# The first scan's causal convolution on TensorE instead of VectorE, an operand's product moved to GpSimd, and an earlier tail for the scan's last chunk

## Chip, cores and metric

The kernel runs on one core of one Trainium2 chip. The time is the device time of one execution in microseconds, as the median of several runs.

## What is computed

The input x is 32 sequences of 256 tokens of 256 features, all float32. A conditioning block with a recurrent scan is applied first; then two layers of windowed attention and a gated feed-forward follow, and x is added at the end. The change touches only the conditioning block, which per sequence is:

```python
xr, gate = jnp.split(x @ W_in.T, 2, axis=-1)          # 512 channels each
xr = xr + t_emb[:, None, :]
xc = causal_depthwise_conv(xr, W_conv, taps=4) + b_conv
xc = silu(xc)
xn = layernorm(xc) * ln_g + ln_b
Bm, Cm, dt = jnp.split(xn @ W_xproj.T, 3, axis=-1)     # 16 states each
dt = jnp.tanh(dt @ W_dt.T + b_dt) * 0.01
Ad = 1.0 + dt * (-jnp.tanh(A_log))
Bd = Bm * jnp.minimum(norm(xn), 1.0)
def step(h, inputs):                                   # 256 steps, one after the other
    ad, bd, xt, ct = inputs
    h = jnp.clip(h * ad[:, :, None] + bd[:, :, None] * xt[:, None, :], -10.0, 10.0)
    return h, jnp.einsum('bd,bdh->bh', ct, h)
y = ys.transpose(1, 0, 2) + D * xn
return y * silu(gate) @ W_out.T
```

## The kernel before, in words

**Groups and the mix.** The sequences are worked on in four groups of eight (`GB = 8`). The scan of group 0 runs first, with no attention beside it; the code calls this `alone`. After it, the attention and feed-forward of group g run beside the scan of group g+1, and the last group's attention runs with no scan beside it.

**Slots.** A group's scan is written as an agenda: `at(s, what, ...)` puts a piece of work into slot s, and slot t holds step t of the scan. Work for a chunk c of 32 tokens (`CH = 32`, so eight chunks) is placed relative to `s0 = 32 c`: its projection at s0-40 and on, `conv_in`, `conv_taps` and `conv_out` of its four channel blocks at s0-38 to s0-29, the layer norm around s0-24, the figures (decay, input and output factors) at s0-11 to s0-5, and the output of chunk c after its steps. The four channel blocks' convolutions of chunk c+1 therefore lie between six slots before the first step of chunk c and its step 3. The agenda gives the order in which instructions are recorded; a scheduler with a model of its own then orders each engine's queue, and each queue runs in order.

**One step.** For step t the row of xn is spread over 128 partitions (16 states x 8 sequences) into a tile `xrep` of two tokens. In the first scan two tokens of four are spread by TensorE (`bx`, L632) and two are read by a DMA (L624); in later groups all are read by DMA. ScalarE multiplies by `beta` (L643), VectorE makes the clipped sum into a new state tile `h` (L650, 512 elements wide), and TensorE sums the states for the output (`y`, L662, four steps at a time). The three `xrep` buffers (`xp`, `bufs=3`) tie a load to the step three tiles earlier.

**The convolution.** `conv_in` (L428) adds the condition to the projection in PSUM and writes `xr` (L437, VectorE); GpSimd makes tap 0 with the bias, `acc` (L443). `conv_taps` (L451) adds taps 1 to 3 by three VectorE operations in place (L454) and ScalarE takes the tanh (L459). `conv_out` writes `xc` (L464, VectorE). `figures` (L551) makes its matmul operand `rhs` on VectorE (L558), twice for each chunk.

**The output.** After the last step of a half chunk (`hb`), `gated` (L711) adds the skip, `out_turn` (L717) transposes on TensorE, `out_gate` (L731) multiplies by the gate, `project_y` (L740) makes eight products, `copy_y` (L751) and `put_y` (L760) store into DRAM scratch `ys`. Attention starts when `load_res` (L864) has read `ys` back.

**PSUM.** All matmul results come from one pool of eight banks (`ps_w`, tag `w`).

**The hand-over.** The last lines of `program` record the scan up to slot S + 17 (`DRAIN = 17`), then the eight `load_res`, then six projections of the first sequence with one more slot each; from there scan slots are dealt out over the attention's stages by a formula that starts from the slot reached (`s0`) and ends at slot 2S + 17.

Of the kernel before, what the change touches and what calls it, by code (L numbers as in the profile page):

```python
# [35 lines left out]
TAPS = 4  # L36
# [16 lines left out]
def bc(ap, axis, n):  # L53

    ap = ap.unsqueeze(axis)
    shape = list(ap.shape)
    shape[axis] = n
    return ap.broadcast_to(shape)
# [15 lines left out]
def kernel(  # L74
# [29 lines left out]
    nc = tc.nc  # L104
# [33 lines left out]
    wc_sb = loaded(w_conv, [P, NC_, TAPS], "wc_sb")  # L138
    bconv_sb = loaded(b_conv, [P, NC_], "bconv_sb")
# [5 lines left out]
    ident = const.tile([P, P], FP, tag="ident", name="ident")  # L145
# [10 lines left out]
    tok_step = sums("tok_step", CH, ident.rearrange("p (b t) -> p t b", b=BJ))  # L156
# [6 lines left out]
    for j in range(NJ):  # L163
# [18 lines left out]
        out=mask_t[:, 0:W], in_=mask_t[:, 0:W], compare_op=ALU.is_ge, fill=MASKED_LOW,  # L182
# [3 lines left out]
        out=mask_t[:, W : 2 * W], in_=mask_t[:, W : 2 * W], compare_op=ALU.is_ge,  # L186
# [29 lines left out]
    for i in range(2):  # L216
        t = const.tile([P, NI * (P + GB)], FP, tag=f"ly{i}", name=f"ly{i}")
# [3 lines left out]
    def program(ctx, exact):  # L221
        rpool = ctx.enter_context(tc.tile_pool(name="res", bufs=1, reuse_waits="tile"))
        wpool = ctx.enter_context(tc.tile_pool(name="weights", bufs=1, reuse_waits="tile"))
        sp = ctx.enter_context(tc.tile_pool(name="sp", bufs=1, reuse_waits="tile"))
# [8 lines left out]
        def bank(pool, tag, name):  # L233
            return pool.tile([P, DI], FP, tag=tag, name=name)
# [150 lines left out]
        def group_scan(g):  # L385
# [7 lines left out]
            b0 = g * GB  # L393
            alone = g == 0

            agendas = [{}]
            state = {"p": one}
            ck = [{} for _ in range(NCH)]

            def at(s, what, *args):  # L400
                agendas[-1].setdefault(s, []).append(partial(what, *args))
# [26 lines left out]
            def conv_in(c, ch):  # L428
                if ch == 0:
                    ck[c]["xc"] = sp.tile([P, NC_, GB * CH], FP, tag="xc", name="xc")  # L430
                ps = ck[c].pop(("ps", ch))
                xr = sp.tile([P, GB, TAPS - 1 + CH], FP, tag="xr", name="xr", bufs=2)
                if c == 0:
                    nc.gpsimd.memset(xr[:, :, 0 : TAPS - 1], 0.0)
                else:
                    nc.gpsimd.tensor_copy(xr[:, :, 0 : TAPS - 1], ck[c - 1]["carry"][:, ch])
                nc.vector.tensor_add(  # L437
                    xr[:, :, TAPS - 1 :],
                    ps.rearrange("p (b t) -> p b t", b=GB),
                    bc(cond_sb[:, ch, b0 : b0 + GB], 2, CH),  # L440
                )
                acc = sp.tile([P, GB, CH], FP, tag="acc", name="acc", bufs=2)
                nc.gpsimd.tensor_scalar(  # L443
                    acc, xr[:, :, 0:CH], wc_sb[:, ch, 0:1], bconv_sb[:, ch : ch + 1],
                    ALU.mult, ALU.add,
                )
                if c < NCH - 1:
                    nc.gpsimd.tensor_copy(ck[c]["carry"][:, ch], xr[:, :, CH:])
                ck[c]["xr", ch] = xr, acc

            def conv_taps(c, ch):  # L451
                xr, acc = ck[c]["xr", ch]
                for k in range(1, TAPS):
                    nc.vector.scalar_tensor_tensor(  # L454
                        acc, xr[:, :, k : k + CH], wc_sb[:, ch, k : k + 1], acc,
                        ALU.mult, ALU.add,
                    )
                th = sp.tile([P, GB * CH], FP, tag="th", name="th", bufs=2)
                nc.scalar.activation(th, acc.rearrange("p b t -> p (b t)"), AF.Tanh, scale=0.5)  # L459
                ck[c]["th", ch] = th  # L460

            def conv_out(c, ch):
                _, acc = ck[c].pop(("xr", ch))
                nc.vector.scalar_tensor_tensor(  # L464
                    ck[c]["xc"][:, ch], ck[c].pop(("th", ch)), 1.0,
                    acc.rearrange("p b t -> p (b t)"), ALU.add, ALU.mult,
                )


# [81 lines left out]
            def figures(c):  # L551
                stat = ck[c].pop("stat")
                pst = bank(ps_w, "w", "ps_st")[:, 0 : 3 * CH].rearrange(
                    "p (i t) -> p i t", i=3
                )
                for j in range(NJ):
                    rhs = sm.tile([P, 3, CH], FP, tag="rhs", name="rhs")
                    nc.vector.tensor_mul(rhs, bc(tok_step, 1, 3), bc(stat[:, j], 2, CH))  # L558
                    nc.tensor.matmul(
                        pst,  # L560
                        sel[:, j].rearrange("p n b -> p (n b)"),
                        rhs,
                        start=(j == 0),
                        stop=(j == NJ - 1),
                    )
                ck[c]["pst"] = pst
# [208 lines left out]
                )  # L775
                rep_w.append(t)

            rep_w = []
            at(-1, start)
            if alone:  # L780
                at(-30, spread_weights)
                constants(at)
            for c in range(NCH):
                for t in range(CH):
                    at(c * CH + t, step, c, t)
            for c in range(NCH):
                s0 = c * CH
                for hb in range(CH // TB):
                    s = s0 + hb * TB
                    for i in range(NI):  # L790
                        at(s + 4 * i + 5, read_out, c, hb, i)
                    at(s + 21, gated, c, hb)
                    at(s + 24, out_gate, c, hb)
                    at(s + 11, skip, c, hb)
                for ch in range(NC_):
                    at(s0 - 38 + 2 * ch, conv_in, c, ch)
                    at(s0 - 37 + 2 * ch, conv_taps, c, ch)
                    at(s0 - 35 + 2 * ch, conv_out, c, ch)
                for ch, s in enumerate((13, 16, 17, 18)):
                    at(s0 + s + 1, gate_th, c, ch)  # L800
                    at(s0 + s + 2, gate_out, c, ch)
                at(s0 - 24, raw_copy, c)
                at(s0 - 23, raw_turn, c)
                for j in range(NJ):
                    s = s0 - 24 + 4 * j
                    at(s + 2, norm_stats, c, j)
                    at(s + 4, norm_apply, c, j)
                    at(s + 5, norm_affine, c, j)
                    at(s + 8, norm_out, c, j)
                at(s0 - 11, length, c)  # L810
                at(s0 - 7, figures_in, c)
                at(s0 - 5, decays, c)
                at(s0 - 4, put_c, c, 0)
                at(s0 + 4, put_c, c, 1)
                for d in range(KM):
                    at(s0 + 44 + 2 * d, copy_y, c, d)
                    at(s0 + 45 + 2 * d, put_y, c, d)
            agendas.append({})
            for c in range(NCH):
                s0 = c * CH  # L820
                at(s0 - 43, load_x, c)
                for ch in range(NC_):
                    at(s0 - 40 + 2 * ch, project, c, ch)
                for ch, s in enumerate((13, 16, 17, 18)):
                    at(s0 + s, project, c, NC_ + ch)
                at(s0 - 26, raw_sums, c)
                for j in range(NJ):
                    at(s0 - 24 + 4 * j, norm_turn, c, j)
                at(s0 - 9, figures, c)
                for t in range(CH):  # L830
                    if t % XR == 0:
                        at(s0 + t - 5, load_rows, c, t)
                    if by_tensor(t) and t % XR == 0:
                        at(s0 + t - 4, spread_rows, c, t)
                    at(s0 + t - 2, scale_row, c, t)
                for hb in range(CH // TB):
                    s = s0 + hb * TB
                    at(s - 9 if alone else s + 7, load_skip, c, hb)
                    at(s + 22, out_turn, c)
                for d in range(KM):  # L840
                    at(s0 + 42 + 2 * d, project_y, c, d)

            return agendas

# [507 lines left out]
        def scan_to(s):  # L1352
            while done[0] is None or done[0] < s:
                done[0] = next(scan, 1 << 30)


        DRAIN = 17
        for i, (kind, k) in enumerate(WEIGHTS):
            scan_to(100 + 8 * i)
            load_weights(0, kind, k)  # L1360
        scan_to(S + DRAIN)
        for b in range(GB):
            load_res(0, b)
        for w in range(NW):
# [135 lines left out]
```

## Time and profile before

| what | value |
|---|---|
| median of 3 runs | 3995.38 us (3995.34, 3995.38, 4005.80) |
| the profiled execution | 4008.98 us |
| its span in the profile | 4007.1 us |
| TensorE busy over the span | 3794.7 us (95%) |
| VectorE busy | 2634.7 us (66%) |
| ScalarE busy | 2327.0 us (58%) |
| GpSimd busy | 1758.9 us (44%) |

The profile's rows name an engine (PE is TensorE, PEld its weight loads, DVE VectorE, ACT ScalarE, POOL GpSimd, SP the engine whose queue issues most DMAs), a source line, the operation, output tile <- input tiles, and a count. In a table of stages each pair `a (xn)` is busy microseconds and instructions of one engine; the last three columns are the clock granted to TensorE, the share of DMA time, and GB/s. A float32 matmul leaves two records, so a count of 8 is four matmuls; a transpose leaves one. A row of the timeline starts with its start and its length in microseconds, and merges equal instructions that follow each other, so its length can hold idle time.

### The profile page before, as it was taken

How to read it: one execution, taken by the hardware profiler on the slowest of the kernel's cores; microseconds unless marked ns; L12 is line 12 of the kernel's file. 1: busy time of each engine (PE TensorE's matmuls, PEld its weight loads, DVE VectorE, ACT ScalarE, POOL GpSimd, SP SyncE). 2: the span in 40 equal slices, each digit the busy share in tenths (PEclk: the TensorE clock that was granted, in tenths of full speed). 3: DMA queues.
4: the chain of work that ended last, by engine and by line, in shares of the span. 5: the costliest groups of instructions: out<-in, count | busy, mean ns of one | idle time of the engine just before them, and what ended most of it. 6: DMA issues, size and time to landing. Idle time of an engine off the chain costs nothing.

```text
span 4007.1 us, 57108 instructions
## 1 busy us (share of the span) xinstructions
PE 3794.7 (95%) x20540; PEld 2375.0 (59%) x20540; DVE 2634.7 (66%) x5241; ACT 2327.0 (58%) x3895; POOL 1758.9 (44%) x1784
## 2 busy tenths in 40 slices
PE   7888889999999899999999999999999999999999
PEld 3333345666666565666666666666666666666666
DVE  6888877777777666676676767666666544444443
ACT  3555546666666566666666666656666554455453
POOL 4443365444444444454444445444444444334341
PEclk8899989999999999999999999999999999999999
DMA  5444543333433435333343444333343111000000
GB/s 151 111 115 114 147 120 95 99 103 99 118 104 99 119 101 123 90 86 102 85 113 98 109 114 120 100 77 102 95 106 98 43 32 44 1 16 20 20 11 23
DMA packets 295896, 353.43 MB, mean 88 GB/s; under 512 B 166627, under 2 KB 213044, under 8 KB 295476
## 3 DMA queue, kind: packets, MB, share of 16 engines
q1 hardware_dynamic: 211154, 337.68, 31.9%
q10 hardware_dynamic: 84450, 12.01, 2.0%
q8 instruction: 165, 2.70, 0.3%
q14 instruction: 127, 1.04, 0.1%
HBM read 314.49 MB, written 33.55 MB: 87 GB/s over the span
## 4 chain that ended last, share of the span: by engine, by line
PE 55%; DVE 8%; POOL 7%; ACT 6%; DMA 5%; issue 3%; ACTq 0%; SPq 0%; POOLq 0%; DVEq 0%
PE ps_qkv L893 11%; PE pa L1224 9%; PE po_f L1247 8%; DMA xrep<-xnd 5%; PE ov L1137 4%; PE sc L1099 3%; PE ps_wo L943 3%; PE y L662 3%; DVE h L650 2%; PE ps_in L407 2%; PE rb L1152 2%; PE rs L1118 2%; POOL rn L925 2%; PE tr_qk L932 2%; PE ps_out L740 1%
## 5 line engine op out<-in xcount | busy, mean ns | idle before, releaser
L650 DVE CUSTOM_DVE_ANT_0 h<-h,xrep,lim 128x512 f32<-128x512 f32 x1024 | 926.3, 905 | 87.1 <-ACT xrep L643 31.8
L643 ACT ACTIVATE xrep<-xrep,beta 128x512 f32<-128x512 f32 x896 | 613.6, 718 | 546.0 <-DMA xrep<-xnd 455.9
L893 PE MATMUL ps_qkv<-qkv,res 128*128 128x512 f32 x1536 | 709.8, 598 | 1.7 <-DMA res<-ys 1.5
L1224 PE MATMUL pa<-hT,w 128*128 128x256 f32 (+1 forms) x3072 | 692.5, 387 | 2.3 <-ACT xn L527 1.7
L917 POOL TENSOR_TENSOR rot<-rot,swp 128x512 f32<-128x512 f32 x256 | 334.0, 1305 | 757.2 <-DVE swp L914 604.5
L1224 PEld LDWEIGHTS pa<-hT,w 128*128 128x128 f32 (+1 forms) x3072 | 498.2, 178 | 210.8 <-issue 68.4
L925 POOL TENSOR_TENSOR rn<-ss,neg_half 128x8 f32<-128x8 f32 x256 | 439.7, 1718 | 23.6 <-DVE ss L923 13.0
L893 PEld LDWEIGHTS ps_qkv<-qkv,res 128*128 128x128 f32 x1536 | 277.3, 190 | 273.6 <-issue 244.9
L1235 DVE SCALAR_TENSOR_TENSOR ag<-pa,b_sb,ag 128x256 f32<-128x256 f32 (+1 forms) x448 | 212.5, 475 | 298.1 <-ACT ag L1232 296.1
L662 PE MATMUL y<-h,ly 128*32 128x512 f32 x2048 | 367.3, 623 | 25.2 <-DVE h L650 23.1
L1247 PE MATMUL po_f<-ag,w 128*128 128x256 f32 (+1 forms) x1536 | 382.4, 390 | 2.0 <-DVE ve L1185 1.3
L1247 PEld LDWEIGHTS po_f<-ag,w 128*128 128x128 f32 (+1 forms) x1536 | 276.5, 189 | 112.2 <-issue 54.5
L926 POOL TENSOR_TENSOR rot<-rot,rn 128x512 f32<-128x512 f32 x256 | 291.4, 1138 | 19.7
L407 PE MATMUL ps_in<-xg,w_in_sb 128*128 128x256 f32 x1024 | 287.7, 409 | 11.1 <-DMA xg<-in_xT_dram 11.0
L1108 ACT ACTIVATE pT<-sc 128x512 f32<-128x512 f32 x384 | 208.3, 594 | 145.4 <-PE sc L1099 144.1
L407 PEld LDWEIGHTS ps_in<-xg,w_in_sb 128*128 128x128 f32 x1024 | 186.5, 196 | 161.9 <-issue 80.1
L909 DVE TENSOR_TENSOR rot<-ps_qkv,rc_sb 128x512 f32<-128x512 f32 x256 | 175.8, 687 | 152.7 <-ACT sq L906 152.5
L454 DVE SCALAR_TENSOR_TENSOR acc<-xr,wc_sb,acc 128x256 f32<-128x256 f32 x384 | 189.5, 495 | 101.4 <-POOL acc L443 99.9
L1108 ACT ACT_TABLE_LOAD x186 | 238.6, 1283 | 19.0 <-PE sc L1099 12.9
L1232 ACT ACT_TABLE_LOAD x187 | 239.9, 1283 | 6.4 <-issue 2.1
L943 PE MATMUL ps_wo<-oT,wo 128*128 128x256 f32 x1024 | 232.0, 380 | 0.0
L1099 PE MATMUL sc<-qT,kT 64*128 64x128 f32 (+1 forms) x2048 | 219.6, 343 | 0.0
(149 smaller groups left out, 5601.7 us busy)
## 6 DMA issues: line engine op xcount, KB each, us to landing
xrep<-xnd SPq DMA_DIRECT2D x448, 512.0 KB
xnd<-xn SPq DMA_DIRECT2D x64, 256.0 KB
qkv<-in_wqkv_dram SPq DMA_DIRECT2D x24, 512.0 KB
xd<-xnd SPq DMA_DIRECT2D x192, 64.0 KB
w<-in_w_dram SPq DMA_DIRECT2D x80, 128.0 KB
xg<-in_xT_dram SPq DMA_DIRECT2D x64, 128.0 KB
ys<-yo ACTq DMA_DIRECT2D x64, 128.0 KB
res<-ys SPq DMA_DIRECT2D x32, 256.0 KB
```

What stands on the lines that cost most here:

```text
L407: nc.tensor.matmul(ps, w_in_sb[:, k, ch * P : (ch + 1) * P], ck[c]["xg"][:, k], start=(k == 0), stop=(k == KM - 1),)
L643: nc.scalar.activation(bx, ck[c].pop(("bx", t), bx), AF.Copy, scale=ck[c]["beta"][:, t : t + 1])
L650: nc.vector._custom_dve(TENSOR_ADD_SAT, out=h_new, in0=state["h"], in1=bx, s0=ck[c]["lim"][:, 0, t : t + 1], s1=ck[c]["lim"][:, 1, t : t + 1],
L662: nc.tensor.matmul(ck[c]["y", hb][32 * q : 32 * q + 32, :], ly[hb % 2][:, 32 * t : 32 * t + 32], ck[c].pop(("h", hb * TB + t)), start=(i = ...
L893: nc.tensor.matmul(ps, res[b][:, k, t0 : t0 + W], wt["qkv", a][:, k], start=(k == 0), stop=(k == KM - 1),)
L917: nc.gpsimd.tensor_add(rot, rot, swp)
L925: nc.gpsimd.tensor_tensor(rn, ss, neg_half, ALU.pow)
L943: nc.tensor.matmul(po[:, d], wt["wo", 0][:, c, d * P : (d + 1) * P], oT[:, c, :], start=(c == 0), stop=(c == NC_ - 1),)
L1099: nc.tensor.matmul(banks[r][:, i, :], kT[rows, i0 + i, kw * W : (kw + 1) * W], qT[rows, i0 + i, kw * W :], start=False, stop=(i == n - 1),)
L1108: nc.scalar.activation(p, banks[r], AF.Exp)
L1224: nc.tensor.matmul(pg if x else pa, wt["w1", m][:, k, x], self.h[:, k], start=(k == 0), stop=(k == KM - 1),)
L1247: nc.tensor.matmul(self.po[:, d], wt["w2", 0][r0 : r0 + n, m, d * P : (d + 1) * P], self.ag[m][r0 : r0 + n], start=(m == 0), stop=(m == le ...
```

## The change

Four things are changed.

1. In the first scan only (`alone`), `conv_taps` becomes five accumulating matmuls into a PSUM bank: one of a row of biases with a row of ones, and one for each of four taps, whose weights are a 128 x 128 diagonal of that tap's 128 channel weights. The tanh and `conv_out` read the PSUM bank. GpSimd's tap 0 and VectorE's three taps are gone there; `acc` has no SBUF tile. The diagonals are built once, by two VectorE products of 1024 elements (`tap_weights`); the bias row is loaded by a DMA of 512 single elements on ScalarE's queue and the ones by a GpSimd memset (`tap_bias`). They live in the buffers of the three `qkv` weights.
2. In all groups, `rhs` is made by GpSimd.
3. For the last half of the last chunk of the first scan (`end`), `gated`, `out_turn`, `out_gate`, `project_y`, `copy_y` and `put_y` are placed 3 to 9 slots earlier, and the eight `load_res` are recorded after slot S + 7 instead of S + 17.
4. The weights are loaded in another order: `wo`, `w1`, `w2` recorded from slot 64 on, the three `qkv` at slot S - 30, because their buffers hold the diagonals until then.

```diff
+            def end(c, hb):
+                return alone and c == NCH - 1 and hb == CH // TB - 1
...
-                acc = sp.tile([P, GB, CH], FP, tag="acc", name="acc", bufs=2)
-                nc.gpsimd.tensor_scalar(
-                    acc, xr[:, :, 0:CH], wc_sb[:, ch, 0:1], bconv_sb[:, ch : ch + 1],
-                    ALU.mult, ALU.add,
-                )
+                if alone:
+                    acc = None
+                else:
...
             def conv_taps(c, ch):
-                xr, acc = ck[c]["xr", ch]
-                for k in range(1, TAPS):
-                    nc.vector.scalar_tensor_tensor(
-                        acc, xr[:, :, k : k + CH], wc_sb[:, ch, k : k + 1], acc,
-                        ALU.mult, ALU.add,
-                    )
+                xr, acc = ck[c].pop(("xr", ch))
+                if alone:
+                    acc = bank(ps_w, "w", "ps_conv")[:, 0 : GB * CH]
+                    nc.tensor.matmul(
+                        acc,
+                        tap_w[2][0:1, 0, ch * P : (ch + 1) * P],
+                        tap_w[2][0:1, 1, 0 : GB * CH], start=True, stop=False
+                    )
+                    for k in range(TAPS):
+                        nc.tensor.matmul(
+                            acc.rearrange("p (b t) -> p b t", b=GB),
+                            tap_w[ch // KM][:, ch % KM, k * P : (k + 1) * P],
+                            xr[:, :, k : k + CH],
+                            start=False,
+                            stop=(k == TAPS - 1),
+                        )
+                else:
...
-                    nc.vector.tensor_mul(rhs, bc(tok_step, 1, 3), bc(stat[:, j], 2, CH))
+                    nc.gpsimd.tensor_mul(rhs, bc(tok_step, 1, 3), bc(stat[:, j], 2, CH))
...
+            def tap_weights(i):
+                t = wpool.tile([P, KM, DI], FP, tag=f"qkv{i}", name="tap_w")
+                nc.vector.tensor_mul(
+                    t.rearrange("p c (k n) -> p c k n", k=TAPS),
+                    bc(bc(ident, 1, TAPS), 1, KM),
+                    bc(wc_sb[:, i * KM : (i + 1) * KM], 3, P),
+                )
+                tap_w.append(t)
+            def tap_bias():
+                t = wpool.tile([P, KM, DI], FP, tag="qkv2", name="tap_b")
+                nc.scalar.dma_start(
+                    out=t[0:1, 0].rearrange("p (c n) -> p c n", c=NC_),
+                    in_=b_conv.rearrange("p c -> c p").unsqueeze(0),
+                )
+                nc.gpsimd.memset(t[0:1, 1], 1.0)
+                tap_w.append(t)
...
+                for i in range(NC_ // KM):
+                    at(-41, tap_weights, i)
+                at(-41, tap_bias)
...
-                    at(s + 21, gated, c, hb)
-                    at(s + 24, out_gate, c, hb)
+                    at(s + (21, 18)[end(c, hb)], gated, c, hb)
+                    at(s + (24, 19)[end(c, hb)], out_gate, c, hb)
...
-                    at(s0 + 44 + 2 * d, copy_y, c, d)
-                    at(s0 + 45 + 2 * d, put_y, c, d)
+                    at(s0 + (44 + 2 * d, 37 + d)[end(c, 1)], copy_y, c, d)
+                    at(s0 + (45 + 2 * d, 37 + d)[end(c, 1)], put_y, c, d)
...
-                    at(s + 22, out_turn, c)
+                    at(s + (22, 18)[end(c, hb)], out_turn, c)
...
-                    at(s0 + 42 + 2 * d, project_y, c, d)
+                    at(s0 + (42 + 2 * d, 36)[end(c, 1)], project_y, c, d)
...
-        for i, (kind, k) in enumerate(WEIGHTS):
-            scan_to(100 + 8 * i)
+        for i, (kind, k) in enumerate(WEIGHTS[3:] + WEIGHTS[:3]):
+            scan_to(S - 30 if kind == "qkv" else S // 4 + 8 * i)
             load_weights(0, kind, k)
-        scan_to(S + DRAIN)
+        scan_to(S + 7)
```

More of the change, by code (lines that the diff above doesn't have):

```diff
@@ L441, in conv_in @@
                 )
-                acc = sp.tile([P, GB, CH], FP, tag="acc", name="acc", bufs=2)
-                nc.gpsimd.tensor_scalar(
-                    acc, xr[:, :, 0:CH], wc_sb[:, ch, 0:1], bconv_sb[:, ch : ch + 1],
-                    ALU.mult, ALU.add,
-                )
+                if alone:
+                    acc = None
+                else:
+                    acc = sp.tile([P, GB, CH], FP, tag="acc", name="acc", bufs=2)
+                    nc.gpsimd.tensor_scalar(
+                        acc, xr[:, :, 0:CH], wc_sb[:, ch, 0:1], bconv_sb[:, ch : ch + 1],
+                        ALU.mult, ALU.add,
+                    )
                 if c < NCH - 1:
@@ L451, in conv_taps @@
             def conv_taps(c, ch):
-                xr, acc = ck[c]["xr", ch]
-                for k in range(1, TAPS):
-                    nc.vector.scalar_tensor_tensor(
-                        acc, xr[:, :, k : k + CH], wc_sb[:, ch, k : k + 1], acc,
-                        ALU.mult, ALU.add,
-                    )
+                xr, acc = ck[c].pop(("xr", ch))
[5 more added lines that the diff above has]
+                        tap_w[2][0:1, 1, 0 : GB * CH], start=True, stop=False
+                    )
+                    for k in range(TAPS):
[7 more added lines that the diff above has]
+                else:
+                    for k in range(1, TAPS):
+                        nc.vector.scalar_tensor_tensor(
+                            acc, xr[:, :, k : k + CH], wc_sb[:, ch, k : k + 1], acc,
+                            ALU.mult, ALU.add,
+                        )
+                    acc = acc.rearrange("p b t -> p (b t)")
                 th = sp.tile([P, GB * CH], FP, tag="th", name="th", bufs=2)
-                nc.scalar.activation(th, acc.rearrange("p b t -> p (b t)"), AF.Tanh, scale=0.5)
-                ck[c]["th", ch] = th
+                nc.scalar.activation(th, acc, AF.Tanh, scale=0.5)
+                ck[c]["th", ch] = th, acc
             def conv_out(c, ch):
-                _, acc = ck[c].pop(("xr", ch))
+                th, acc = ck[c].pop(("th", ch))
                 nc.vector.scalar_tensor_tensor(
-                    ck[c]["xc"][:, ch], ck[c].pop(("th", ch)), 1.0,
-                    acc.rearrange("p b t -> p (b t)"), ALU.add, ALU.mult,
+                    ck[c]["xc"][:, ch], th, 1.0, acc, ALU.add, ALU.mult
                 )
@@ L776, in spread_weights @@
                 rep_w.append(t)
-            rep_w = []
+            def tap_weights(i):
[11 more added lines that the diff above has]
+                    in_=b_conv.rearrange("p c -> c p").unsqueeze(0),
+                )
+                nc.gpsimd.memset(t[0:1, 1], 1.0)
+                tap_w.append(t)
+            rep_w, tap_w = [], []
             at(-1, start)
```

## The prediction, as put on record

> **What bounds the kernel now.** I read the table of stages first, to see where the kernel has idle time (columns: span, busy time and count of PE, PEld, DVE, ACT, POOL; granted clock, DMA share, GB/s):
>
> ```profile
> 47.00:98.00 51.00, 46.90 (x153) 17.21 (x153) 44.70 (x89) 28.44 (x53) 23.83 (x30) 0.94 0.47 128
> 199.50:250.30 50.80, 45.09 (x172) 18.09 (x172) 43.23 (x81) 29.06 (x55) 21.68 (x33) 0.90 0.45 115
> 301.00:352.00 51.00, 45.67 (x172) 18.09 (x172) 43.98 (x81) 28.55 (x54) 19.93 (x25) 0.90 0.45 114
> 900.00:1300.00 400.00, 386.83 (x2208) 249.32 (x2207) 295.74 (x582) 256.11 (x433) 182.92 (x189) 1.00 0.41 105
> 3260.00:4007.00 747.00, 738.68 (x4224) 509.12 (x4222) 309.02 (x684) 362.05 (x567) 275.49 (x235) 1.00 0.07 19
> ```
>
> From about 600 us to the end TensorE is busy 97 to 99% of the time and bounds the kernel; nothing taken from VectorE is worth anything there. The first scan (53 to 460 us) is different. One of its chunks of 32 steps takes 50.8 us (189 steps in 300 us), and PE and DVE are both busy 85 to 90%. The chain that ended last shows nothing ahead of 640 us, so I look at the groups of instructions of 150 to 450 us, shapes kept apart:
>
> ```profile
> L650 DVE CUSTOM_DVE_ANT_0 h<-h,xrep,lim 128x512 f32<-128x512 f32 x189 | 162.2, 858 | 13.6 <-ACT xrep L643 6.7 <-PE ps_out L740 1.0
> L662 PE MATMUL y<-h,ly 128*32 128x512 f32 x378 | 101.5, 645 | 6.9 <-DVE h L650 5.9
> L454 DVE SCALAR_TENSOR_TENSOR acc<-xr,wc_sb,acc 128x256 f32<-128x256 f32 x70 | 34.1, 488 | 7.3 <-POOL acc L443 7.3
> L443 POOL TENSOR_SCALAR acc<-xr,wc_sb,bconv_sb 128x256 f32<-128x256 f32 x23 | 29.9, 1300 | 45.0 <-DVE xr L437 44.7
> L558 DVE TENSOR_TENSOR rhs<-tok_step,stat 128x96 f32<-128x96 f32 x11 | 8.8, 832 | 0.0
> L607 POOL TENSOR_TENSOR ly<-ct,st_seq 128x128 f32<-128x128 f32 x12 | 7.8, 651 | 6.2 <-PE y L662 5.7
> L643 ACT ACTIVATE xrep<-xrep,beta 128x512 f32<-128x512 f32 x94 | 63.9, 718 | 31.9 <-DMA xrep<-xnd 31.9
> ```
>
> PE's 90% is not work alone: `y` is busy for 101 us because it waits for the next `h` between its matmuls. The waits of 0 to 450 us (total, times, longest) have it, and two stretches of the timeline (start, length) show where:
>
> ```profile
> PEld y L662 <- DVE h L650: 56.1, 51, 2.5
> ```
>
> ```profile
> 213.61 4.34 PE L662 MATMUL y<-h,ly 128*32 128x512 f32 x8 [1.08 <-DVE h L650]
> ...
> 220.34 1.13 PE L632 MATMUL bx<-xq,rep_w 32*128 32x512 f32 x4
> 221.40 0.66 PE L503 MATMUL tp_x<-ident,xc 128*128 128x128 f32 x4
> 221.98 1.05 PE L662 MATMUL y<-h,ly 128*32 128x512 f32 x4
> 222.97 3.72 PE L740 MATMUL ps_out<-zT,w_out_sb 128*128 128x256 f32 x16
> 226.62 1.13 PE L632 MATMUL bx<-xq,rep_w 32*128 32x512 f32 x4
> ...
> 228.26 1.07 PE L662 MATMUL y<-h,ly 128*32 128x512 f32 x8
> 229.26 1.99 PE L407 MATMUL ps_in<-xg,w_in_sb 128*128 128x256 f32 x8
> ```
>
> Each row from 220.34 on starts where the one before ends: from 217.9 to 237.9 us, 20 us of each chunk, PE has no wait, and 14 steps pass at 1.34 us. In the other 30.8 us, where the convolutions lie, 18 steps take 1.71 us each, four `y` that need 1.07 us take 4.34 us, and PE waits for DVE. So the first scan has a PE-limited and a DVE-limited stretch, and the change moves work from DVE to PE in the second.
>
> [...] the eight `ps_out` matmuls of 256 columns take 3.65 us to the next start, 0.456 each[...]. [...] `rhs` has a median of 253 ns in the mixed part, but 832 ns on average here, where a GpSimd product of 1.26 us starts 0.06 us ahead of it.
>
> **The change, part by part.** The sum is made against the profiled execution's own 4008.98 us (span 4007.1 and 1.9 around it), which lies 13.6 us above the median of 3995.38; the difference is then taken from the median.
>
> *Taken from DVE, per chunk.* Twelve `acc` of 0.488 us: 5.86, less about 0.09 each that overlaps its neighbours: 4.8. Their wait for GpSimd's `acc`: 7.3 us in 5.9 chunks, 1.2. Two `rhs`: 1.48 us in the timeline, 1.4. Sum 7.4 us. GpSimd loses four `acc` (5.2 us) and gains two `rhs`. Their GpSimd time isn't in the trace: at least the 0.25 us that DVE needs, at most the 0.65 of the larger `ly` product; I take 0.5. GpSimd was busy 20 of 51 us and has room; the product now directly follows the GpSimd power that it needs, so no hand-over is added.
>
> *Put on PE, per chunk.* Four groups of five matmuls of 256 columns: 20 x 0.43 = 8.6 us. PE's own work per chunk, from start to start in the timeline: 16 `bx` in pairs of 1.06, 8 `y` groups of 0.99, 8 `ps_in` of 0.97, `ps_out` 3.65, `ps_raw` 1.87, transposes 2.4, `ps_st` 1.1: 33.2 us; 41.8 after. The 20 us stretch is PE-limited already and gets none of either. The other has 13.2 us of PE work before and 21.8 after; with a clock of 0.95, between the 0.90 of here and the 1.00 of the busy part, 23 us. DVE's need there falls from 30.8 to 23.4. The two are level, so waits between them now show. In the changed order on PE a channel's projection stands one or two groups ahead of its convolution, with DVE's `xr` between: up to one `h` (0.8) and `xr` (0.42) and hand-overs, less the bias matmul (0.43), about 0.8 us each, 3.2 per chunk (bounds 0 and 8.6: nothing, or every group in full). 23.4 + 3.2 = 26.6, and the chunk is 46.6: 4.2 us less, of at most 7.4. Queued behind a waiting convolution are `bx` and `y`; who waits for them is ScalarE's scaling, two slots later, then the step. The tanh and `xc` read PSUM instead of SBUF; I take no change. The group's bank comes from the eight in use; its own wait for a bank is within the 3.2.
>
> *How often.* Chunks 1 to 7 have their convolution beside steps: 7 x 4.2 = 29.4. Chunk 0's is in the start-up, and beside chunk 7 lies group 1's, which stays on DVE; there only `rhs` goes: 1.4.
>
> *Start-up.* Two DVE products of 1024 elements[...]. DVE has nothing to do from about 7 to 13.5 us, waiting for x: hidden[...]. The bias DMA is behind four others on ScalarE's queue, is issued near 9 us, and is needed at 13.9 us: hidden if it lands within 4 us. Chunk 0 itself trades 12 `acc` for 20 matmuls at a clock of 0.76: 8.6/0.76 = 11.3 us on PE against 14 us from the first `xr` to the last `xc` before, PE's other work coming on top: I take 2 us lost (from -2 to +6).
>
> *Weights.* The `qkv` loads (1.5 MB) were issued at 10 us and now stand in SP's queue among the `xrep` loads of the last chunks. An `xrep` load of 512 KB lands 4.7 to 5.2 us after issue. Behind three such loads one load may be late by up to 8 us; I take 2 us lost (0 to 8). `wo`, `w1`, `w2` still lead the queue.
>
> *Tail.* Before, the last `ys` store is issued at 483.6, the first `res` load at 487.6, the first `ps_qkv` at 491.2. The order on DVE has 278 steps ahead of the first attention product before, 270 after. Eight steps of 1.55 us come off: 12.4. They are done later, in the PE-bound part, at (33.2 - 8.5 for `bx`)/32 = 0.77 us of PE each: 6.2 back. Net 6.2 (0 to 12).
>
> *Mixed part.* `rhs` on GpSimd for 24 more chunks: DVE isn't the bound there, GpSimd is under half busy; taken as 0.
>
> Sum: 29.4 + 1.4 - 2 - 2 + 6.2 = 33 us. The profiled execution would be 3976, the median **3962 us**.
>
> **Rivals.** *DVE's relief passes in full* (no waits between the two): 7 x 7.4 + 1.4 - 4 + 6.2 = 55: 3940. [...] Against: 21.8 us of matmuls in a stretch of 23.4. *PE or the row loads take the place of DVE* (the clock stays at 0.90; or `xrep` lands later: issue, 5 us to land and 0.72 to scale must fit in five steps, 1.2 us a step, near the 1.34 of the fast stretch): some 2.2 us a chunk: 19 us, 3976. *Given back in the mixed part*: a `rhs` behind one GpSimd `rot` product (1.3 us) in each of 24 chunks, with PE standing at `ps_st`: 31 us, 3993. Against: PE's waits there for `ps_st` were 3.8 us in all. *Slower*: each of the 28 groups holds the step loop by its full length, 2.15 us, a bank's 0.84 and a hand-over, 3.2 us: 28 x 3.2 - 51.8 = 38 lost, less 3.6 for tail and rest: 4030. It decides from 2.0 us a group on. Against: `bx` is made two slots ahead of its scaling. That the convolution isn't moved can be left out: the built order has it on PE.
>
> **Numbers.** Chances: forecast 0.42, full relief 0.17, half 0.20, given back 0.12, slower 0.09. Outside 3930 to 3990 lie a tenth of the first and some of full relief (together 4%), half of "given back" and all of "slower": 19%. A measurement of this kernel tells about 0.3%, 12 us, from no change. Faster by more: 0.75; within: 0.15; slower: 0.10.
>
> **What would show it.** In the table of stages a chunk of the first scan near 46.6 us with PE above 90% and DVE near 80%; `y`'s wait for `h` well under 56 us; new waits of `ps_conv` for `xr` of about 0.8 us; the first `ps_qkv` near 450 us; `rhs` on GpSimd near 0.5 us; the mixed part within 10 us of before. A chunk at 43 or at 49, a hole at the `qkv` loads, or a longer mixed part would prove the matching step wrong.

## The result, and the profile after

The changed kernel takes 4047.4 us (median of four runs, 4045.2 to 4056.9) against 3999.2 for the kernel before in the same session. These medians are 48 us apart; the ratio estimated from all runs is 1.0114, with a 95% interval of 1.0099 to 1.0130. It is slower by 1.1%, some 46 us, where 33 us less was forecast. The profiled execution has a span of 4043.3 us, 36.2 more than before.

Two landmarks split these 36.2 us: the second `zT` of each chunk, and the first `tp_h` of each attention sequence (one of 64, read in the timeline).

| us | before | after | more |
|---|---|---|---|
| first `zT` (start-up and first half chunk) | 87.9 | 98.7 | 10.8 |
| one chunk, mean of seven | 51.1 | 52.2 | 1.15 |
| last `zT` of the first scan | 471.9 | 492.1 | 20.2 |
| first `ps_qkv` | 491.2 | 507.8 | 16.6 |
| first `tp_h` | 608.6 | 613.6 | 5.0 |
| from there to the 13th sequence's `tp_h` | 703.7 | 747.5 | 43.8 |
| from there to the end | 2694.7 | 2682.2 | -12.5 |

So the scan's chunks got longer in place of shorter, the tail's gain came (16.6 falls to 5.0), and 44 us were lost in 750 us of the mixed part, where I had put nothing but 6 us of returned steps. The last row differs by up to 26 us between the kernels measured here (2675 to 2701); as the sessions differ too, a single one of these tells nothing. Of the seven chunks, the first five hold a convolution on TensorE in the changed kernel; beside the last two lies that of the next group, which stayed on VectorE. And with the earlier tail the last `zT` itself is placed sooner: the last chunk takes 45 to 48 us in the seven kernels that have it, 48 to 50 in the others. The mean of seven therefore shows less than a chunk with the convolution loses.

The table of stages after, in the prediction's stretches (span, then busy time and count of PE, PEld, DVE, ACT, POOL; clock, DMA share, GB/s):

```profile
47.00:98.00 51.00, 42.54 (x164) 21.71 (x164) 31.76 (x59) 25.33 (x49) 17.49 (x25) 0.87 0.43 111
199.50:250.30 50.80, 44.46 (x204) 23.34 (x204) 38.60 (x66) 26.92 (x51) 17.21 (x29) 0.90 0.44 115
900.00:1300.00 400.00, 371.32 (x2035) 236.28 (x2033) 272.07 (x527) 245.68 (x417) 174.60 (x176) 0.97 0.42 106
```

These stretches have a fixed length and hold fewer steps after than before. The five chunks with the convolution, whole, from the second `zT` to the twelfth, before and after:

```profile
114.28:372.41 258.13, 229.95 (x861) 91.00 (x862) 220.94 (x406) 145.87 (x270) 104.06 (x133) 0.89 0.45 113
126.48:393.37 266.89, 234.78 (x1062) 119.63 (x1061) 204.92 (x336) 145.54 (x270) 85.38 (x124) 0.90 0.44 115
```

A chunk of these takes 51.6 us before and 53.4 after. VectorE is busy 44.2 us of it and then 41.0, so 3.2 us of work have gone; but it stands idle for 12.4 us in place of 7.4. Neither engine is full. In 900 to 1300 us TensorE has lost 15 us of busy time and 3% of its clock. The groups of 150 to 450 us:

```profile
L674 DVE CUSTOM_DVE_ANT_0 h<-h,xrep,lim 128x512 f32<-128x512 f32 x179 | 166.2, 928 | 30.9 <-PE y L686 12.2 <-ACT xrep L667 12.0 <-DVE h L674 2.0
L469 PE MATMUL ps_conv<-xr,tap_w 128*128 128x256 f32 x160 | 39.9, 391 | 0.0
L463 PE MATMUL ps_conv<-tap_b 1*128 1x256 f32 x40 | 13.9, 426 | 0.0
L489 DVE SCALAR_TENSOR_TENSOR xc<-th,ps_conv 128x256 f32<-128x256 f32 x20 | 8.4, 420 | 15.1 <-ACT th L484 15.1
L582 POOL TENSOR_TENSOR rhs<-tok_step,stat 128x96 f32<-128x96 f32 x12 | 5.1, 447 | 0.5
L583 PE MATMUL ps_st<-rhs,sel 128*128 128x96 f32 x24 | 7.0, 448 | 27.2 <-POOL rhs L582 27.2
```

`h` ran 189 times before and 179 after; its idle time has gone from 13.6 to 30.9 us, 12.2 of it until TensorE has read an old `h` (no such wait before) and 12.0 until ScalarE has scaled the row (6.7 before). Every one of these rows in the five chunks was spread by TensorE (`bx`); no step waited for a row read by DMA. `xc` now waits 15 us for the tanh of `ps_conv`; before, it didn't wait. `rhs` takes the half us that was forecast. TensorE's idle time has gathered at `ps_st`, 27 us (9.2 before). Of the waits of 0 to 450 us, that of `y` has fallen from 56.1 to 16.1, and that of `ps_st` has grown (`ps_st` before and after, then `y` after):

```profile
PE ps_st L559 <- DVE rhs L558: 13.4, 8, 2.8
PE ps_st L583 <- POOL rhs L582: 33.5, 8, 5.0
PEld y L686 <- DVE h L674: 16.1, 17, 1.8
```

The mean `h` has grown from 858 to 928 ns. Most take 0.81 us in both kernels, and every one above 0.85 us overlaps a GpSimd product, as here in the changed kernel:

```profile
259.67 1.79 DVE L674 CUSTOM_DVE_ANT_0 h<-h,xrep,lim 128x512 f32<-128x512 f32 x1
259.62 1.29 POOL L716 TENSOR_TENSOR xd<-xq,dskip_sb 128x512 f32<-128x512 f32 x1
```

In the kernel before it was `rhs` that met this `xd`. What the long `h` take above 0.81 us is 1.9 us a chunk in the five chunks before, 2.4 in e1 below (only `rhs` moved), 3.2 in e3 (only the convolution moved) and 4.2 in the changed kernel. So 2.3 us of what VectorE was relieved of came back as longer `h`.

### The profile page after: what moved, and what is told of

The parts are those of the page before. It is cut to its first block, busy times and chain, and to the rows that moved or that the text cites. A ratio compares the mean times of both kernels' runs of the same rounds, so it can differ in the third digit from the quotient of the medians.

```text
span 4043.3 us, 57661 instructions
## 1 busy us (share of the span) xinstructions
PE 3815.3 (94%) x20860; PEld 2425.6 (60%) x20860; DVE 2595.9 (64%) x5083; ACT 2326.0 (58%) x3895; POOL 1743.3 (43%) x1817
## 4 chain that ended last, share of the span: by engine, by line
PE 53%; DVE 13%; DMA 11%; POOL 9%; ACT 9%; issue 4%; ACTq 0%; SPq 0%; POOLq 0%; DVEq 0%
DMA xrep<-xnd 10%; PE ps_qkv L940 10%; PE pa L1271 8%; PE po_f L1294 7%; DVE h L674 5%; PE ov L1184 4%; PE ps_in L412 3%; PE y L686 3%; PE sc L1146 3%; POOL rn L972 3%; ACT xrep L667 2%; PE ps_wo L990 2%; PE rs L1165 2%; PE tr_qk L979 2%; PE rb L1199 2%
## 5 line engine op out<-in xcount | busy, mean ns | idle before, releaser
L674 DVE CUSTOM_DVE_ANT_0 h<-h,xrep,lim 128x512 f32<-128x512 f32 x1024 | 947.8, 926 | 134.8 <-ACT xrep L667 49.5
L1294 PEld LDWEIGHTS po_f<-ag,w 128*128 128x128 f32 (+1 forms) x1536 | 276.7, 189 | 112.3 <-issue 56.1
L686 PE MATMUL y<-h,ly 128*32 128x512 f32 x2048 | 303.9, 623 | 10.8 <-DVE h L674 10.6
L412 PE MATMUL ps_in<-xg,w_in_sb 128*128 128x256 f32 x1024 | 295.1, 416 | 13.5 <-DMA xg<-in_xT_dram 10.8
L953 ACT ACTIVATE sq<-ps_qkv 128x512 f32<-128x512 f32 x256 | 150.3, 592 | 119.1 <-PE ps_qkv L940 34.8
```

The source lines that it names most:

```text
L412: nc.tensor.matmul(ps, w_in_sb[:, k, ch * P : (ch + 1) * P], ck[c]["xg"][:, k], start=(k == 0), stop=(k == KM - 1),)
L674: nc.vector._custom_dve(TENSOR_ADD_SAT, out=h_new, in0=state["h"], in1=bx, s0=ck[c]["lim"][:, 0, t : t + 1], s1=ck[c]["lim"][:, 1, t : t + 1],
L686: nc.tensor.matmul(ck[c]["y", hb][32 * q : 32 * q + 32, :], ly[hb % 2][:, 32 * t : 32 * t + 32], ck[c].pop(("h", hb * TB + t)), start=(i = ...
L1294: nc.tensor.matmul(self.po[:, d], wt["w2", 0][r0 : r0 + n, m, d * P : (d + 1) * P], self.ag[m][r0 : r0 + n], start=(m == 0), stop=(m == le ...
```

## Experiments

The kernel before took 4003 to 4019 us in the five sessions of the experiments; so ratios are given, each to the kernel before in the same session. Chunks are the mean of seven as above; kernels whose first scan is the same differ by up to 0.7 us in that column (e5 and e10).

| kernel | ratio to before (95%) | chunk | first `tp_h` | to the 13th |
|---|---|---|---|---|
| changed | 1.0114 (1.0099 to 1.0130) | 52.2 | 613.6 | 747.5 |
| e1 rhs on GpSimd | 0.9980 (0.9973 to 0.9987) | 50.1 | 607.5 | 704.3 |
| e2 changed, rhs on VectorE | 1.0159 (1.0139 to 1.0179) | 53.2 | 622.6 | 761.3 |
| e3 convolution only | 1.0074 (1.0055 to 1.0094) | 53.8 | 639.2 | 709.9 |
| e4 tail and loads | 1.0096 (1.0078 to 1.0114) | 50.8 | 597.9 | 762.9 |
| e5 the same, old pace | 1.0024 (1.0015 to 1.0032) | 50.5 | 624.4 | 709.9 |
| e6 new pace only | 1.0091 (1.0073 to 1.0108) | 51.3 | 597.3 | 758.1 |
| e7 e3 without bias | 0.9981 (0.9968 to 0.9993) | 50.7 | 609.0 | 706.5 |
| e8 rhs, tail, old pace | 1.0009 (1.0000 to 1.0018) | 49.6 | 619.0 | 707.0 |
| e9 e7, ScalarE's bias, rhs | 0.9953 (0.9928 to 0.9978) | 49.0 | 597.4 | 711.6 |
| e10 e4, late steps | 1.0032 (1.0018 to 1.0045) | 51.2 | 594.6 | 739.7 |
| e11 e9, `ps_st` later | 0.9917 (0.9895 to 0.9939) | 46.9 | 579.5 | 710.9 |
| e12 longer drain | 1.0069 (1.0047 to 1.0092) | 51.4 | 626.1 | 726.4 |
| e13 `ps_st` later only | 0.9953 (0.9937 to 0.9968) | 49.2 | 602.2 | 708.5 |
| e14 changed, two mended | 0.9969 (0.9955 to 0.9984) | 48.1 | 599.2 | 708.9 |
| e15 e11, 3 of 4 groups | 0.9930 (0.9911 to 0.9950) | 47.8 | 582.0 | 708.7 |
| e16 rhs, `ps_st` later | 0.9970 (0.9956 to 0.9984) | 49.7 | 606.4 | 711.3 |
| e17 e11, two slots later | 0.9917 (0.9900 to 0.9935) | 46.9 | 580.3 | 710.6 |

**Which part loses.** From the 27 us of standing at `ps_st` I first blamed GpSimd's `rhs` (theory A); the rival was the convolution (B), and for the mixed part the moved steps (C).

e1, on the kernel before:

```diff
-nc.vector.tensor_mul(rhs, bc(tok_step, 1, 3), bc(stat[:, j], 2, CH))
+nc.gpsimd.tensor_mul(rhs, bc(tok_step, 1, 3), bc(stat[:, j], 2, CH))
```

> The kernel before with one line changed: the two rhs products of a chunk on GpSimd. Theory A (the product on GpSimd is what costs: TensorE stands at ps_st until GpSimd delivers, with bx, y and ps_in queued behind): some 3 us in each of 7 chunks of the first scan and about half a us in each of 24 chunks beside the attention, 25 to 40 us slower than before. Theory B (the convolution on TensorE is what costs, the line is harmless): within 8 us of before, PE's wait for rhs near 10 us in the first 450 us.

e2, the same line turned back in the changed kernel:

> The changed kernel with only the rhs products put back on VectorE. Theory A: 25 to 40 us less than the changed kernel, so within 20 us of the kernel before; chunk of the first scan near 50 us. Theory B: within 8 us of the changed kernel, that is some 48 us slower than before.

e3, on the changed kernel, with `rhs` turned back as well:

```diff
-return alone and c == NCH - 1 and hb == CH // TB - 1
+return False
...
-scan_to(S + 7)
+scan_to(S + DRAIN)
```

> The convolution of the first scan on TensorE alone (with the late qkv loads that its operands' place forces): rhs on VectorE, the old distances of the last chunk's output and the old drain of 17 steps. Theory A: 10 us lost in the start-up, a chunk 0 to 3 us shorter than before, so -10 to +10 us against before. Theory B: a chunk as in the changed kernel (52 us), 25 to 45 us slower than before.

e4, on the changed kernel, `rhs` turned back and the convolution taken through the old branch (its diagonals are not built):

```diff
-if alone:
+if False:
```

> The shorter distances for the last chunk's output, the start of the first attention ten steps earlier and the late qkv loads alone: convolution and rhs as before. By the prediction's terms for tail and weights 4 us faster than before (12.4 of steps, half of it given back, 2 for the loads). Rival C (the ten steps that move beside the attention cost more there than in the scan, so the loss after 500 us is theirs): the first ps_qkv 8 to 12 us earlier, but 5 to 20 us slower than before in all.

Theory A falls: `rhs` on GpSimd is a gain alone (0.2%) and in the changed kernel (e2 is slower by 0.45% of before, 18 us, which neither of its forecasts had). With `rhs` on VectorE, e3 stands at `ps_st` just as long:

```profile
259.80 1.14 PE L583 MATMUL ps_st<-rhs,sel 128*128 128x96 f32 x4 [5.42 <-DVE rhs L582]
```

The convolution loses 0.7% and the tail 1.0%, in different places: e3 in its chunks (2.7 us each) and 8 us ahead of them, with the mixed part near that of before; e4 between the first and the 13th sequence, 59 us, after gaining at the first.

**The tail's loss is the pace.** The steps of the other groups' scan are dealt out among the attention's stages by `s0 + (2 * S + DRAIN - s0) * (t + 1) // reload`, and `s0` is where the scan stood. A drain shorter by ten steps thus deals 260 steps over 114 stages in place of 250, and moves every one of them.

e5 (on e4, the first edit) and e6 (on the kernel before, the second) change this alone:

```diff
-s0 = done[0]
+s0 = S + DRAIN + 3 * NW
...
-s0 = done[0]
+s0 = S + 7 + 3 * NW
```

> The tail-and-loads kernel, but from the first stage of attention on the steps of the scan are dealt out as in the kernel before: the twelve outstanding steps at once, then 250 over 114 stages in place of 260. Theory C1 (the pace at which steps are dealt among the attention's stages costs the 59 us between the first and the twelfth sequence): the loss goes, 10 us faster than before to 5 slower. Theory C2 (it is something else of the tail, or the late loads): still 25 to 40 us slower than before.

> The kernel before with one change: steps dealt out among the attention's stages as the changed kernel does (260 over 114 stages counted from step 269; the first four stages get none, since the old drain has done them). Tail, loads, convolution and rhs as before. Theory C1: 35 to 60 us slower than before, all of it between the first and the twelfth sequence. Theory C2: within 8 us of before.

e6 has the loss without the tail, e5 the tail without most of the loss. But e5 is still 8 us slower than before, outside its forecast, and e8 (e5 with `rhs` on GpSimd), for which I had forecast 8 to 18 us less than before, comes out level. At the old pace the twelve outstanding steps are made up ahead of the first `tp_h`, which comes 16 us later than before in e5; so the earlier tail gains nothing there. The stage tables from the first to the 13th sequence, of the kernel before, of e6 and of e5, in this order:

```profile
609.00:1312.00 703.00, 676.17 (x3832) 436.80 (x3830) 522.10 (x1027) 446.21 (x751) 330.22 (x338) 0.99 0.40 102
```

```profile
597.60:1355.00 757.40, 694.43 (x3868) 443.88 (x3866) 536.05 (x1046) 458.85 (x777) 328.12 (x341) 0.97 0.39 99
```

```profile
624.70:1334.00 709.30, 678.07 (x3832) 438.36 (x3830) 524.51 (x1027) 445.54 (x751) 331.61 (x338) 0.99 0.40 101
```

e6 spends 54 us more: 18 as PE's busy time (36 more of 3832 matmul records, 1%, and a clock of 0.97 for 0.99, 2%) and 36 as idle time (63 against 27). TensorE's longest wait there is for VectorE's sum of the residual; of e6, 597 to 1361 us:

```profile
PE tp_h L1177 <- DVE res L951: 40.4, 12, 7.1
```

In the same window of the kernel before that is 28.0 us; but the weight loads ahead of these products waited 24.7 us for the same sum there and 10.9 in e6, so what the added idle time waits for isn't settled. New is a wait of `tr_qk` for ScalarE's `pT`, 8.0 us.

Which property of the pace does it? e10 (on e4, the first edit) keeps the old rate from the new start, e12 (on the kernel before, the second) takes a lower rate:

```diff
-scan_to(s0 + (2 * S + DRAIN - s0) * (t + 1) // reload)
+scan_to(s0 + (2 * S + DRAIN - s0 - (12 if t + 1 < reload else 0)) * (t + 1) // reload)
...
-scan_to(S + DRAIN)
+scan_to(S + DRAIN + 10)
```

> The tail-and-loads kernel (260 steps from step 269 on), dealt out at 2.18 a stage as in the kernel before (2.19), the twelve that are missing all at the last of the 114 stages. The steps then stand at the phases of the attention at which the slow kernel begins, but at the old rate. Rate theory (2.28 steps a stage is too dense): 0 to 15 us slower than before, the loss at the end. Phase theory (it is where in a sequence the heavy items of a chunk fall): 30 to 55 us slower, spread over the first twelve sequences.

> The kernel before with ten more steps done ahead of the attention: 240 over 114 stages, 2.11 a stage. Rate theory, straight line: 16 us lost ahead of the attention, up to 50 won in it: 20 to 35 us faster than before. Rate theory with a threshold above 2.19: 5 to 10 us slower than before (16 lost, 8 of TensorE's work won). Phase theory: anything, and not spread evenly over the sequences.

Neither theory holds alone. e10 has the old rate and loses 36 us: 15 in the first sequence, 2 in the next eight, 19 in the last three. So the level middle speaks for the rate and the two ends against it. And e12's lower rate loses too, 19 us in its first four sequences. All thirteen kernels that deal the steps as before (the kernel before is one of them) take 704 to 712 us, with whatever else changed; the other six take 726 to 763. That it is the pace is shown; what makes the old one good is not, and stays open.

**The convolution's loss is TensorE's.** The changed kernel's timeline of PE in a chunk:

```profile
259.41 1.17 PE L583 MATMUL ps_st<-rhs,sel 128*128 128x96 f32 x4 [4.97 <-POOL rhs L582]
260.51 2.08 PE L656 MATMUL bx<-xq,rep_w 32*128 32x512 f32 x4
262.52 2.08 PE L412 MATMUL ps_in<-xg,w_in_sb 128*128 128x256 f32 x4
264.52 1.94 PE L686 MATMUL y<-h,ly 128*32 128x512 f32 x8
266.39 1.39 PE L412 MATMUL ps_in<-xg,w_in_sb 128*128 128x256 f32 x4
267.71 0.69 PE L463 MATMUL ps_conv<-tap_b 1*128 1x256 f32 x2
268.33 2.00 PE L469 MATMUL ps_conv<-xr,tap_w 128*128 128x256 f32 x8
270.26 1.13 PE L656 MATMUL bx<-xq,rep_w 32*128 32x512 f32 x4
271.31 1.13 PE L412 MATMUL ps_in<-xg,w_in_sb 128*128 128x256 f32 x4
...
307.43 0.63 PE L741 MATMUL tz<-ident,xd 128*128 128x128 f32 x4 [1.80 <-DVE xd L735]
312.56 1.17 PE L583 MATMUL ps_st<-rhs,sel 128*128 128x96 f32 x4 [4.50 <-POOL rhs L582]
```

From the first `ps_st` on each row starts where the one before ends: TensorE never waits among the convolutions, and VectorE waits for it, directly at `y` and `ps_in` or through ScalarE at `xc` and the `bx` rows. Then, once a chunk, TensorE stands 5 us at `ps_st`, and the 6 us after that stand run at half rate (`bx` takes 2.01 us to the next start at 260.51, and 1.05 at 270.26). A convolution takes 267.71 to 270.26 = 2.55 us, of which 0.62 is the bias. Theory D: TensorE bounds the chunk. Rival E: the chain round the figures does.

e7, on e3, leaves the convolution's bias out:

```diff
-nc.tensor.matmul(
-    acc,
-    tap_w[2][0:1, 0, ch * P : (ch + 1) * P],
-    tap_w[2][0:1, 1, 0 : GB * CH], start=True, stop=False
-)
...
-start=False,
+start=(k == 0),
```

> The kernel with only the convolution on TensorE, without the fifth matmul of each group: the convolution's bias is left out of the first group's scan. Theory D (TensorE is the bound of the first scan now): 4 x 0.6 us less in each of 7 chunks, 15 to 20 us faster than with the bias, so about 10 us slower than before. Theory E (a chain of waits round the figures of the next chunk sets the chunk, TensorE only stands in it): at most 5 us less than with the bias.

Theory D, and by more than expected: 3.0 us a chunk in the mean of seven, 21 in all, and the first `zT` at 90.2 after 95.8. The four bias matmuls of a chunk are 2.5 us, and only five of the seven chunks have them; the rest of the gain isn't accounted for. The longer `h` don't decide: over the five chunks e7 still has 2.9 us of them, of e3's 3.2, and its chunk of 51.1 is down at the 51.6 of before, from e3's 54.8. e9 then computes all of it: on e7, with `rhs` on GpSimd as in e1, and

```diff
+biased = sp.tile([P, GB * CH], FP, tag="acc", name="biased", bufs=2)
+nc.scalar.activation(biased, acc, AF.Identity, bias=bconv_sb[:, ch : ch + 1])
+acc = biased
```

> Convolution on TensorE with four matmuls a group, its bias added by ScalarE on the way out of PSUM (computed in full), rhs on GpSimd, old tail and old pace. Theory D (TensorE bounds the first scan, the fifth matmul was the loss): as without the bias, less 5 to 15 us for rhs: 12 to 25 us faster than before. Theory E (the chain of waits sets the chunk): the second pass on ScalarE lengthens it by 0.4 us in each of 28 groups: no better than before, up to 10 us slower.

Theory D again. To test the stand at `ps_st`, e11 puts it one slot later in e9 (the first edit; it holds for all four groups), e13 in the kernel before and e16 in e1; e17 has `figures` at `s0 - 7` and, by the second edit, its reader one slot later too:

```diff
-at(s0 - 9, figures, c)
+at(s0 - 8, figures, c)
...
-at(s0 - 7, figures_in, c)
+at(s0 - 6, figures_in, c)
```

> As the kernel with ScalarE's bias, and ps_st one slot later in TensorE's order. If TensorE's stand at ps_st (4.7 to 5.4 us a chunk) is time lost: 1 to 2 us a chunk, 7 to 14 us less than without the shift. If the chain behind it (decays, first row of the next chunk) is the limit: no gain, 0 to 10 us more.

> The kernel before with ps_st one slot later in TensorE's order and nothing else. If the stand at ps_st (9 us in 250 here, against 23 with the convolution on TensorE) is a loss only where TensorE bounds the scan: within 6 us of before. If it is a loss anyway: 8 to 15 us faster than before.

> The kernel before with rhs on GpSimd and ps_st one slot later, the convolution on VectorE. If the convolution on TensorE (with four matmuls a group) is worth nothing even so: 0.7 to 0.9% faster than before, as with it. If it is worth 0.5 to 1 us a chunk: 0.4 to 0.65% faster.

> As the kernel with ps_st one slot later (convolution on TensorE, bias on ScalarE, rhs on GpSimd), with ps_st and what reads it one slot later still. If TensorE's stand is what is left to gain: another 1 us a chunk, some 1.0% faster than before. If the chain from ps_st to the next chunk's first step is the limit by then: no better than one slot, 0.5 to 0.8% faster than before.

The slot is worth 2.1 us a chunk with the convolution on TensorE (e9 to e11) and 1.9 without (e13), so the stand is a loss in either kernel. As the slot moves in the later groups too, and the part after the 13th sequence takes 2675 to 2689 us in the five kernels that have it and 2678 to 2701 in the others, some of the ratio may come from there; no run parts the two. e11's timeline shows how in the first scan:

```profile
274.52 1.13 PE L656 MATMUL bx<-xq,rep_w 32*128 32x512 f32 x4
278.33 1.08 PE L583 MATMUL ps_st<-rhs,sel 128*128 128x96 f32 x4 [2.68 <-POOL rhs L582]
279.20 1.97 PE L412 MATMUL ps_in<-xg,w_in_sb 128*128 128x256 f32 x4
```

`bx` now stands ahead of `ps_st`, so ScalarE and the steps have their rows while TensorE waits, and the stand is 2.7 us. e11's chunk of 46.9 us is what I had forecast for the changed kernel, for reasons that it lacked. e17 gains no more. e16 falls short of e13 (chunk 49.7 against 49.2, within the spread, and the first `zT` at 96.1 against 92.2; it is at 97.1 and 97.7 in e1 and e8 too, whose `rhs` is also on GpSimd beside the old convolution; why stays open). Between e16 and e11 the only difference is the convolution (four matmuls, ScalarE's bias, and the late loads that its operands' place forces): 0.5%. Against e13, the best without it, e11 and e17 gain 0.36%. So on TensorE it is a gain once the fifth matmul and the early `ps_st` are gone.

e15 takes the last channel group of e11 off TensorE:

```diff
-if alone:
+if alone and ch < NC_ - 1:
```

> As the kernel with ps_st one slot later, but the convolution of the last of the four channel groups back on VectorE. If TensorE is still the bound there: 1.9 us of it less in each chunk, up to 10 us faster than with all four. If the two engines are level: within 5 us. If VectorE is the bound again: 5 to 10 us slower than with all four.

The engines are about level: e15 is 0.1% slower than e11, inside the intervals.

e14 mends just the two failed steps in the changed kernel, with e9's bias and e5's pace:

> The changed kernel with its two failed steps mended: no fifth matmul (the bias added by ScalarE), and the old pace of steps. Tail, late loads and rhs as changed. If the two are the whole loss: 19 us gained as in the kernel with ScalarE's bias, 8 to 10 given back by tail and loads with the burst of twelve steps: 5 to 15 us faster than before. If something else of the changed kernel costs: slower than before.

As expected: the two account for the whole loss. The best versions measured are e11 and e17, 0.8% faster than before.

## Why the prediction was wrong, point by point

- **DVE's relief of 7.4 us a chunk** came only in part. 6.2 of it was work, and VectorE is busy 3.2 us less in a chunk (44.2 to 41.0), since `h` itself took 2.3 us more beside GpSimd's products; the prediction had seen that delay for `rhs` and did not ask what `xd` would meet once `rhs` had left. `rhs` on GpSimd was priced right (0.447 us) and gave 0.9 to 1.0 us a chunk (before to e1, e2 to changed, e5 to e8), near the spread but three times the same way, for the 1.4 put down. Rival three, `rhs` costing in the mixed part, fell: e1 takes 704.3 there, before 703.7.
- **"23.4 + 3.2 = 26.6, and the chunk is 46.6"** is the first step that failed; its 23.4 rests on the full relief. I took TensorE's own work as 41.8 us and spread waits over the convolution. The 0.43 us for a matmul of 256 columns was my estimate; the kernel before shows it in the mixed part, where the four `pa` at 1005.92 us take 1.73 us to the next start, but not among the convolutions: a tap took 0.48 and the bias 0.62. Measured from `ps_st` to `ps_st` (259.41 to 312.56): 53.2 us. That is 41.8, and 1.6 because a group takes 2.55 us and not 2.15, and 2.8 for the half rate after the stand (260.51 to 266.39 for what takes 3.1 elsewhere), and 6.3 of standing at `tz` and `ps_st`: 52.5, which leaves 0.7 open. The waits of `ps_conv` for `xr` that I had named did not come (1.7 us in 300, of its weight loads); TensorE was too late for them, and `xc` waited for the convolution (15.1 us in 300). `ps_st`, which I entered with its 1.1 us of work, had a wait before (13.4 us in eight) and I left it out. The half rate (`bx` 2.01 us for 1.05) comes here after a stand of 4.97 us, and after shorter ones too: in e11 after one of 2.68 us (`ps_in` at 279.20 takes 1.90 us to the next start, for 0.97), and in the kernel before after two of 2.61 and 1.86 us with little work between them:

```profile
240.54 0.63 PE L717 MATMUL tz<-ident,xd 128*128 128x128 f32 x4 [2.61 <-DVE xd L711]
244.87 1.14 PE L559 MATMUL ps_st<-rhs,sel 128*128 128x96 f32 x4 [1.86 <-DVE rhs L558]
245.94 2.08 PE L632 MATMUL bx<-xq,rep_w 32*128 32x512 f32 x4
```

- **"7 x 4.2"** counted a chunk too many: chunk 1's convolution begins at 53.9 us, ahead of the first step, so six stand beside steps. And 20 us for 14 steps are 1.43 us each, not 1.34. Both are small.
- **The start-up's 2 us lost** was too small: the first `zT` came 10.8 later. It is at 90.7 to 92.2 in e6, e12 and e13, which start as the kernel before, so 3 to 4 of it is spread between runs. The bias is 5.6 of it by e3 (95.8) and e7 (90.2), and all six kernels with the convolution on TensorE but no bias matmul stand at 89.3 to 92.3, the three with it at 95.8 to 100.2. Its DMA, issued at 9.40, held TensorE until 16.88 (2.2 us idle), where I had allowed it 4 us to land. The two products of the diagonals took 1.22 us each, from 6.42 to 8.78 us, ahead of TensorE's first matmul at 10.77, which waited for x.
- **The loads' 2 us**: no hole; e4's chunk is 50.8.
- **The tail**: 12.4 us were to come off, and from the last `zT` to the first `tp_h` e4 and the changed kernel gained 15. But this gain did not last: **"They are done later ... 6.2 back"** is the second step that failed: the new `s0` re-deals all 250 steps, and the 44 to 59 us lost stand where 6.2 were put.
- **"Mixed part: 0"** held for `rhs`, not for the pace, which I hadn't seen to be in the diff.
- The slower rival had the right sign and the wrong place: in the chunks 8 us were lost, not 38, and the pace cost the rest. The rival that TensorE takes VectorE's place, which I gave 0.20 and a gain of 19 us, was the true one for the chunk; I had priced it at a clock of 0.90 and without its stand. Its other branch, rows that land later, did not come. The full-relief rival did not come either: from 150 to 400 us TensorE is busy 89% at a granted clock of 0.90 in the changed kernel, and was 89% at 0.91 before. In e11 it is busy 94%, at 0.95.
- Two of the signs came true although the forecast was wrong: `y` waits far less for `h`, and `rhs` takes half a us. They show that work left VectorE, not that the chunk gets shorter.

## What to carry to other kernels

When work is moved to another engine, list the waits in its queue first and price what is queued behind each: in the changed kernel `bx` stood behind a `ps_st` that waited 4.97 us, in e11 it was queued ahead and ran before the wait, and this one-slot move was worth about as much as the whole convolution (0.5%). A step count that feeds a planner is not a local edit: look for every later use of the position it leaves. Before moving work to TensorE, keep off it what an engine with time to spare can add (here a bias on ScalarE, busy 29 of 51 us). Where a product leaves one engine, ask which instruction meets its old neighbour next.

## What the hardware showed unexpectedly

The bias matmul, with one row of operands, took 0.62 us to the next start, a tap with 128 rows 0.48. After a stand of 4.97 us TensorE ran at half rate for about 6 us (`bx` 2.01 for 1.05), after one of 2.68 us (e11) for about 3 (`ps_in` 1.90 for 0.97). A VectorE `h` of 0.81 us took 1.79 us where a GpSimd product of 1.29 us began 0.05 us ahead of it. The DMA of 512 single elements to one partition was used 7.5 us after its issue, and took 1.23 us of ScalarE's queue to issue.
